# A transformer block on one core: second batch's first feature tiles moved to the end of attention, key rows prepared a product later, weight sums stored in pieces

## The chip, the cores and the metric

The kernel runs on one core of one Trainium2 chip. The core has a matrix engine (PE, whose weight loads are shown as PEld), a vector engine (DVE), an activation engine (ACT), a general engine (POOL) and a synchronization engine (SP), which here only issues DMAs. Each engine runs its own list of instructions in order and waits on semaphores for the others. DMAs are issued by SP, POOL and, a few, ACT; a DMA is in turn on the list of the engine that issues it. The metric is the device time of one execution in microseconds (us), as the median of several runs.

## The reference

The input x has two batches of 2048 tokens with 576 features; a condition vector per batch gives six modulation vectors. All arithmetic is 32-bit.

```python
mod = jax.nn.silu(c) @ w_ada + b_ada
sh_msa, sc_msa, g_msa, sh_mlp, sc_mlp, g_mlp = jnp.split(mod, 6, axis=1)
xn = _ln(x, 1e-06)
xn = xn * (1 + sc_msa[:, None, :]) + sh_msa[:, None, :]
qkv = (xn @ w_qkv + b_qkv).reshape(B, N, 3, H, hd)      # 16 heads of 36
q, k, v = (qkv[:, :, 0], qkv[:, :, 1], qkv[:, :, 2])
q = _ln(q, 1e-05, qn_g, qn_b)
k = _ln(k, 1e-05, kn_g, kn_b)
attn = softmax(jnp.einsum('bqhd,bkhd->bhqk', q, k) * scale)
o = jnp.einsum('bhqk,bkhd->bqhd', attn, v).reshape(B, N, C)
x = x + g_msa[:, None, :] * (o @ w_proj + b_proj)
xn2 = _ln(x, 1e-06) * (1 + sc_mlp[:, None, :]) + sh_mlp[:, None, :]
x = x + g_mlp[:, None, :] * (gelu(xn2 @ w1 + b1) @ w2 + b2)
```

## The kernel before, in words

Tokens are cut into 16 tiles of 128 per batch. For each batch the program projects the tiles to keys, queries and values (`inputs`), runs attention (`attend`), and projects the outputs (`outputs`); behind both batches comes the two-layer MLP. Where a batch's stage ends and the next begins, PE goes straight on.

**The order of the work.** Inside a `tc.manual_schedule(engines=...)` block the named engines run their instructions in the order in which the Python code writes them. Outside of it a scheduler places instructions, and it may place them into an earlier stage if what they need is there. PE is in written order everywhere in this program. In `inputs` DVE, SP and POOL are (for the second batch ACT too); in `attend` DVE, POOL and ACT; around `outputs` DVE alone.

**Feature tiles.** A token tile is normalized, turned by DVE in squares, stored to DRAM (`turned<-squares`, L1034, on POOL) and loaded back with features on the partitions: `input_loaded` (L1042 and two DMAs at L1044 into `xnt`). `input_modulated` then applies scale and shift: four ACT instructions at L1051, one at L388, one at L389, and a subtraction by POOL at L390. For the second batch the rows are turned during the first batch's attention (`turned_early`, at blocks 14 to 29 of its 32). The first three tiles are loaded behind `attend` with `input_loaded(turned.pop(t), nc.sync)`; two are modulated through a table handed to `outputs`, the third in `in_pairs`. That code stands outside of the written order of ACT and SP.

**First batch's projections.** One tile at a time: three products (L1130, L1132), bias additions on DVE (L1145, L1148), and head norms. Each loop over t loads the features of tile t+2 and turns the rows of tile t+3 on POOL's queue, and stores the transposed queries and keys on SP (L1111). At tiles 6 to 11 it also works off the list `summed`: four differences of weight blocks on DVE (`sum_made`, L961), the last rows' difference (`ends_less`), then both stored to DRAM by SP (`sums_kept`, L971 and L972) for the second batch.

**Second batch's projections** (`in_pairs`). Tiles 0 and 1 are projected as above; then seven loops over pairs of tiles, t0 = 2, 4, ..., 14, each with a key, a query and a value product (`seven_products`, L1216 to L1222). A product has four groups of matmuls, (1), (2, 6), (5, 7), (4, 3), each in a PSUM tile of two banks; four such tiles exist. `combined` gives the evictions: `copied` on ACT (L1245) empties group 1, and five DVE instructions `do[0]` to `do[4]` (L1240 to L1244) empty the others: `do[0]` group (2, 6), `do[1]` and `do[3]` group (5, 7), `do[2]` and `do[4]` group (4, 3). `finishing` makes the head norms: squares on ACT (L1279), sums (L1283), roots, reciprocals (L1290), a product on POOL (L1292), the transpose on DVE (L1296) with eight stores (L1299). Behind the keys of every second pair it issues loads of `km` and `ke`, the key rows for attention (`take_k_block`), and behind the queries of the second pair those of `qm` and `qe`; the four DVE instructions that prepare them (L847 twice, L856, L857) go on the list `taken`, which `rows_made` works off.

**Attention.** 8 pairs of heads, 4 blocks of 512 queries, 4 steps each: scores on PE (L1515), exponentials on ACT (L1519), products with the values on PE (L1528), whose sums DVE adds up (L1578, L1580). `hooks` is a table from a step to work to be done there; what a hook returns is done one step later. The last entry of the loop has the step `(None, None, None)`, when the last exponentials are issued.

**Output projection.** PE at L406 and L417, evictions on DVE (L1657, L1670), loads and stores of residual rows on POOL's queue (L1652, L1671), and ACT computing standard deviations (L276) for the first rows of the MLP.

Of the kernel before, what the change touches and what calls it, by code (L numbers as in the profile page):

```python
# [16 lines left out]
P = 128  # L17
# [14 lines left out]
def dit_block(  # L32
# [719 lines left out]
    def block_of_small():  # L752
# [163 lines left out]
        def first_weights(then):  # L916
# [48 lines left out]
                nc.vector.tensor_tensor(raw_less, rows[:, :, 1, :], rows[:, :, 0, :], ALU.subtract)  # L965
                weight_parts(wq4_less, raw_less)

            def sums_kept():
                saved["sums"] = dram.tile([P, 4, 2, 3, HALF], F32, name="sums_kept")
                saved["less"] = dram.tile([P, 3, HALF], F32, name="less_kept")  # L970
                nc.sync.dma_start(out=saved["sums"], in_=sums)  # L971
                nc.sync.dma_start(out=saved["less"], in_=wq4_less.bitcast(F32))  # L972

            by_head = pool.tile([2 * H, HD], F32, name="by_head")
            nc.gpsimd.dma_start(out=by_head, in_=b_qkv[0 : 2 * C].rearrange("(h d) -> h d", d=HD))
# [17 lines left out]
                nc.sync.dma_start(out=saved["wq"], in_=wq[:, :, 0 : 2 * C])  # L993
                nc.sync.dma_start(out=saved["wq4"], in_=wq4.bitcast(F32))

            summed = [*(lambda i=i: sum_made(i) for i in range(4)), ends_less, sums_kept]
            return (wq, wq4, bq), close, (made, ends_made, bias_made, bias_spread, kept, summed)

        def kept_weights():
# [74 lines left out]
        def inputs(b, weights, making, work, xnts, turned, loaded):  # L1074
# [244 lines left out]
            def in_pairs():  # L1319
# [10 lines left out]
                features_begun(3)  # L1330
                k = product(1, 0)
                biased(1, k, 0)
                input_modulated(b, xnts[2])
                q = product(0, 0)
                biased(0, q, 0)
                v = product(2, 0)
# [17 lines left out]
                for t0 in range(2, NT, 2):  # L1354
# [22 lines left out]
                    if not last:  # L1377
                        for t in range(2):
                            input_modulated(b, xnts[t0 + 2 + t])
                        more = token_sums(t0 + 2)  # L1380
                    do[1]()
                    kt()
                    do[2](), do[3](), do[4]()
                    qs, qr, qq, qd, qt = finishing(0, t0)
# [6 lines left out]
                    qd()  # L1391
                    do[1]()
                    if not last:
                        rows_made()
                        rest = [*do[2:], qt]
                        continue
                    key_rows = [*taken]
                    for ready in key_rows[:-2]:
                        ready()
                    qt()  # L1400
                    do[2](), do[3](), do[4]()
                    return key_rows[-2:]

            modulated = {0}
            done = 0
# [315 lines left out]
        for b in range(B):  # L1721
# [42 lines left out]
            if b + 1 < B:  # L1764
                opening["turned"] = {}
                load, measure, root, turn = rows_ahead(lambda t: x[b + 1, t * P : (t + 1) * P, :])

                def turned_early(t):
                    opening["turned"][t] = turn(t)

                def also(block, g, do):
                    at = (*divmod(block, NBLK), g)
                    before = hooks.get(at)
                    hooks[at] = (lambda: (before(), do())[0]) if before else do

                hooks |= {
                    (0, 2, 1): ada_opened,
                    (1, 0, 2): ada_gates,
                    (2, 0, 2): ada_feature_rows,
                    (2, 0, 3): ada_features,  # L1780
                }
                for t in range(NT):
                    also(3 + t // 2, t % 2, lambda t=t: load(t))
                    also(4 + t // 2, 1 + t % 2, lambda t=t: measure(t))
                    also(14 + t, 0, lambda t=t: load(t))
                    also(14 + t, 1, lambda t=t: turned_early(t))
                also(13, 0, root)
            with tc.manual_schedule(
                engines={mybir.EngineType.DVE, mybir.EngineType.Pool, mybir.EngineType.Activation}
            ):  # L1790
# [4 lines left out]
            wp, close_wp = opening["wp"]  # L1795
            if b + 1 < B:
                weights, close_weights, making = kept_weights()
                turned, loaded = opening["turned"], {}
                xnts = {t: input_loaded(turned.pop(t), nc.sync) for t in range(3)}
                first = []  # L1800

                def turned_of(t):
# [1 line left out]
                    return (lambda x1: first.append(squares_turned(x1, nc.gpsimd, squares))) if t <= TPB else None  # L1804

                with tc.manual_schedule(engines={mybir.EngineType.DVE}):
                    outputs(b, wp, {12 + t: [lambda t=t: input_modulated(b + 1, xnts[t])] for t in range(2)}, spare[:8], turned_of)
                close_wp()
                close_outs()

# [383 lines left out]
```

## Time and profile before

| | us |
|---|---|
| median of 3 runs | 3163.59 |
| lowest, highest | 3161.44, 3164.07 |
| profiled execution | 3168.81 |
| its span, first to last instruction | 3167.0 |
| PE busy in the span | 3114.6 |
| DVE, ACT, POOL busy | 1567.3, 1478.1, 709.5 |
| mean granted TensorE clock | 0.994 |

The first batch's projections run until about 245 us, its attention until about 1046, its output projection until about 1118, the second batch's projections until about 1322, its attention until about 2093, then output projection and MLP.

In a timeline each row gives the start, the duration, the engine, the source line, the operation, what it writes and reads, how often it stands there in a row, and in brackets how long the engine was idle before it and what ended that. "b" and "s" are PSUM tiles. Matmuls are pipelined, so the durations of neighbouring rows overlap; the time that a stretch of matmuls takes is read from its start to the next stretch's start. The granted clock is 1.00 where PE runs at full speed.

### The profile page before, as it was taken

The numbers are of one execution on the slowest core, as the hardware profiler recorded it, in microseconds if no ns is written. First come the engines' busy times: TensorE is split into PE (matmuls) and PEld (weight loads), VectorE is DVE, ScalarE is ACT, GpSimd is POOL, SyncE is SP. The second block draws the span as 40 slices with busy tenths as digits, with TensorE's granted clock in tenths as the row PEclk, the third lists the DMA queues.
The fourth block names the chain that finished last, engine by engine and source line by source line (L and its number), as shares of the span: only waits on it lengthen the run. The fifth ranks groups of instructions, "written<-read, shape, count | busy, mean of one in ns | idle before, by whom it ended". The sixth has DMA issues, their size and how long they took to land. (4 is left out here: it accounts for less than half of the span.)

```text
span 3167.0 us, 46995 instructions
## 1 busy us (share of the span) xinstructions
PE 3114.6 (98%) x17511; PEld 1855.1 (59%) x17511; DVE 1567.3 (49%) x2287; ACT 1478.1 (47%) x2853; POOL 709.5 (22%) x996
## 2 busy tenths in 40 slices
PE   8999999989999999999999999999999999999999
PEld 6874333333333677633333333358888888777777
DVE  6773444434443556544344444345566554445454
ACT  2326666666666123366666666643565552000000
POOL 4650110122321345300001111012333320111121
PEclk9999999989999999999999999999999999999999
DMA  5773332233332554511122222146544434333331
GB/s 145 165 163 85 99 90 60 65 85 96 90 95 77 172 126 76 103 43 36 42 59 74 76 61 74 56 148 193 162 133 138 132 111 157 117 120 112 120 105 39
DMA packets 296039, 324.66 MB, mean 103 GB/s; under 512 B 168856, under 2 KB 227032, under 8 KB 293560
## 3 DMA queue, kind: packets, MB, share of 16 engines
q1 hardware_dynamic: 248096, 199.30, 21.7%
q0 software_dynamic: 46528, 116.94, 14.2%
q10 hardware_dynamic: 1176, 5.31, 0.5%
q8 instruction: 141, 2.31, 0.3%
q14 instruction: 98, 0.80, 0.1%
HBM read 200.50 MB, written 110.43 MB: 98 GB/s over the span
## 5 line engine op out<-in xcount | busy, mean ns | idle before, releaser
L1519 ACT ACTIVATE pt<-b 128x512 f32<-128x512 f32 x2048 | 1057.9, 608 | 490.5 <-PE b L1528 272.3
L1528 PE MATMUL b<-pt,vt 128*64 128x512 f32 x4096 | 943.3, 603 | 17.8 <-ACT pt L1519 17.8
L1528 PEld LDWEIGHTS b<-pt,vt 128*64 128x64 f32 x4096 | 273.7, 137 | 606.0 <-issue 444.1
L1515 PE MATMUL b<-qm,km 32*128 32x512 f32 x4096 | 563.9, 613 | 0.6 <-PE b L1515 0.6
L1580 DVE TENSOR_TENSOR ot<-b,ot 128x512 f32<-128x512 f32 x192 | 132.8, 691 | 613.3 <-PE b L1528 613.3
L1515 PE MATMUL b<-qe,ke 16*128 16x512 f32 x2048 | 420.0, 791 | 0.0
L2106 PE MATMUL s<-ws,as 128*128 128x288 f32 x1440 | 351.8, 406 | 0.0
L1515 PEld LDWEIGHTS b<-qm,km 32*128 32x128 f32 x4096 | 191.0, 184 | 272.4 <-ACT pt L1519 211.5
L2106 PEld LDWEIGHTS s<-ws,as 128*128 128x128 f32 x1440 | 273.6, 190 | 75.6
L1130 PE MATMUL s<-wq,xnt 128*128 128x288 f32 x864 | 230.5, 411 | 6.2 <-ACT xnt L1051 4.2
L1547 DVE RECIPROCAL den<-den 128x512 f32<-128x512 f32 x64 | 213.6, 3337 | 12.5 <-DMA den<-den_dram 12.5
L1946 PE MATMUL m<-xnt,wb 128*128 128x256 f32 x864 | 210.5, 379 | 1.8 <-DVE cs L1980 0.9
L1946 PE MATMUL m<-s,wb 128*128 128x256 f32 x864 | 210.0, 379 | 0.0
L1130 PEld LDWEIGHTS s<-wq,xnt 128*128 128x128 f32 x864 | 160.3, 192 | 43.1 <-ACT xnt L1051 4.4
L1578 DVE COPY ot<-b 128x512 f32<-128x512 f32 x64 | 44.3, 692 | 274.1 <-PE b L1528 274.1
L1946 PEld LDWEIGHTS m<-s,wb 128*128 128x128 f32 x864 | 164.2, 190 | 22.3
L1515 PEld LDWEIGHTS b<-qe,ke 16*128 16x128 f32 x2048 | 106.9, 184 | 113.7 <-issue 113.0
L1946 PEld LDWEIGHTS m<-xnt,wb 128*128 128x128 f32 x864 | 158.8, 190 | 21.8 <-DVE cs L1980 1.5
L1051 ACT ACTIVATE xnt<-xnt,mod 128x128 f32<-128x128 f32 x244 | 100.4, 480 | 128.6 <-DMA xnt<-turned 123.1
L1984 ACT ACTIVATE cs<-cs,b_sb 128x512 f32<-128x512 f32 x144 | 98.9, 719 | 112.9 <-DVE cs L1979 89.2
L1034 POOL DMA_DIRECT2D turned<-squares x160 | 107.5, 679 | 192.8 <-DVE squares L1029 180.7
L2106 PE MATMUL s<-ws,hidden 128*128 128x288 f32 x576 | 142.3, 406 | 0.0
(257 smaller groups left out, 3271.8 us busy)
## 6 DMA issues: line engine op xcount, KB each, us to landing
gelu<-cs SPq DMA_DIRECT2D x144, 256.0 KB
hidden<-gelu SPq DMA_DIRECT2D x16, 2304.0 KB
spare<-in_x_dram POOLq DMA_DIRECT2D x64, 288.0 KB, 3.1
x_dram<-spare POOLq DMA_DIRECT2D x64, 288.0 KB, 2.4
qm<-qk SPq DMA_DIRECT2D x256, 64.0 KB
den<-den_dram SPq DMA_DIRECT2D x128, 128.0 KB
xnt<-turned POOLq DMA_DIRECT2D x53, 256.0 KB, 3.9
turned<-squares POOLq DMA_DIRECT2D x160, 72.0 KB, 2.6
```

What stands on the lines that cost most here:

```text
L1034: queue.dma_start(out=by_square[g], in_=squares[g * SQ : (g + 1) * SQ, :].rearrange("p (k j) -> p k j", j=SQ))
L1051: nc.scalar.activation(part, part, AF.Identity, **affine(which, k, b))
L1130: nc.tensor.matmul(out_a, full[:, k, :], wq[:, k, f], start=k == 0, stop=False)
L1515: nc.tensor.matmul(ps, k[r, keys], q[r, :], start=first, stop=not first)
L1519: nc.scalar.activation(pt[:, h, :], banks[2 * c + h], AF.Exp, scale=SCALE)
L1528: nc.tensor.matmul(acc[64 * h : 64 * h + 64, :], vt[:, v0 : v0 + 64], pt[:, h, :], start=pt is pts[0][0], stop=pt is pts[-1][0],)
L1547: nc.vector.reciprocal(den, den)
L1578: nc.vector.tensor_copy(ot, acc)
L1580: nc.vector.tensor_tensor(ot, acc, ot, ALU.add)
L1946: nc.tensor.matmul(out_m[m], wb[:, slot[m], k, f * P : (f + 1) * P], moving[m](k), start=k == 0 and m in (1, 2, 5, 6), stop=k == 1 and m == 1,
L1984: nc.scalar.activation(part, part, AF.Gelu, bias=b1_sb[:, g : g + 1])
L2106: nc.tensor.matmul(ms[m], stationary[m][:, f, :], ws[m][:, f, :], start=(f == 0), stop=(f == HF - 1))
```

## The change

Three edits.

1. The loads of the second batch's first three feature tiles are written as a hook at the last entry of the first batch's attention, on POOL's queue, and one function modulates all three one step later. They are taken out of the code behind attention and out of `in_pairs`.
2. In `in_pairs`, `rows_made` is called in every pair's query product, ahead of the transpose of the keys, and no longer in the value product. Rows whose loads a pair's key product issues are therefore prepared in the next pair's query product.
3. The weight sums are stored in four DMAs, each written one tile behind the sum that it stores, in place of one DMA behind all of them.

```diff
-            def sums_kept():
-                saved["sums"] = dram.tile([P, 4, 2, 3, HALF], F32, name="sums_kept")
-                saved["less"] = dram.tile([P, 3, HALF], F32, name="less_kept")
-                nc.sync.dma_start(out=saved["sums"], in_=sums)
-                nc.sync.dma_start(out=saved["less"], in_=wq4_less.bitcast(F32))
...
-            summed = [*(lambda i=i: sum_made(i) for i in range(4)), ends_less, sums_kept]
+            saved["sums"] = dram.tile([P, 4, 2, 3, HALF], F32, name="sums_kept")
+            saved["less"] = dram.tile([P, 3, HALF], F32, name="less_kept")
+
+            def sum_kept(i):
+                nc.sync.dma_start(out=saved["sums"][:, i], in_=sums[:, i])
+
+            def less_kept():
+                nc.sync.dma_start(out=saved["less"], in_=wq4_less.bitcast(F32))
+
+            summed = [
+                *(lambda i=i: (sum_made(i), i and sum_kept(i - 1)) for i in range(4)),
+                lambda: (ends_less(), sum_kept(3)),
+                less_kept,
+            ]
...
                 biased(1, k, 0)
-                input_modulated(b, xnts[2])
                 q = product(0, 0)
...
                         more = token_sums(t0 + 2)
                     do[1]()
+                    rows_made()
                     kt()
                     do[2](), do[3](), do[4]()
...
                     qd()
                     do[1]()
                     if not last:
-                        rows_made()
                         rest = [*do[2:], qt]
                         continue
-                    key_rows = [*taken]
-                    for ready in key_rows[:-2]:
-                        ready()
                     qt()
                     do[2](), do[3](), do[4]()
-                    return key_rows[-2:]
+                    return taken
...
+                def features_early():
+                    opening["xnts"] = {t: input_loaded(opening["turned"].pop(t), nc.gpsimd) for t in range(3)}
+                    return [lambda: [input_modulated(b + 1, opening["xnts"][t]) for t in range(3)]]
+
+                hooks[None, None, None] = features_early
...
-                turned, loaded = opening["turned"], {}
-                xnts = {t: input_loaded(turned.pop(t), nc.sync) for t in range(3)}
+                xnts, turned, loaded = opening["xnts"], opening["turned"], {}
...
-                    outputs(b, wp, {12 + t: [lambda t=t: input_modulated(b + 1, xnts[t])] for t in range(2)}, spare[:8], turned_of)
+                    outputs(b, wp, {}, spare[:8], turned_of)
```

The order of instructions shows where the scheduler had put the first edit's work, and where it stands now. ACT in the first batch's attention, before (`pt` are the exponentials):

```order
L1519 ACTIVATE pt<-b 128x512 x48
L1051 ACTIVATE xnt<-xnt,mod 128x128 x4
L388 ACTIVATE xnt_8984<-xnt_8984,mod 128x128
L389 ACTIVATE tail<-xnt_8984,mod 128x128
L1519 ACTIVATE pt<-b 128x512 x32
L1051 ACTIVATE xnt<-xnt,mod 128x128 x4
L388 ACTIVATE xnt_8990<-xnt_8990,mod 128x128
L389 ACTIVATE tail<-xnt_8990,mod 128x128
L1519 ACTIVATE pt<-b 128x512 x32
```

and in the changed kernel (where the exponentials are at L1523 and the modulations at L1059):

```order
L1523 ACTIVATE pt<-b 128x512 x600
L1059 ACTIVATE xnt<-xnt,mod 128x128 x4
L388 ACTIVATE xnt_8963<-xnt_8963,mod 128x128
L389 ACTIVATE tail<-xnt_8963,mod 128x128
L1059 ACTIVATE xnt<-xnt,mod 128x128 x4
L388 ACTIVATE xnt_8969<-xnt_8969,mod 128x128
L389 ACTIVATE tail<-xnt_8969,mod 128x128
L1059 ACTIVATE xnt<-xnt,mod 128x128 x4
```

The three groups of modulations, 32 exponentials apart before, now follow the last exponential of the first batch. POOL's list at that place in the changed kernel (L1042 are the stores of turned rows there, L1050 and L1052 the tiles' loads, L1656 and L1675 the output projection's loads and stores):

```order
L1042 DMA turned_8433<-spare 32x18x32 x4
L1050 DMA xnt<-turned_5079 128x4x128
L1052 DMA xnt_8963<-turned_5079 64x128 x2
L1050 DMA xnt<-turned_5302 128x4x128
L1052 DMA xnt_8969<-turned_5302 64x128 x2
L1050 DMA xnt<-turned_5542 128x4x128
L1052 DMA xnt_8975<-turned_5542 64x128 x2
L1656 DMA spare<-x_dram 128x576
L390 TENSOR_TENSOR xnt_8963<-tail,xnt_8963 128x128
L390 TENSOR_TENSOR xnt_8969<-tail,xnt_8969 128x128
L390 TENSOR_TENSOR xnt_8975<-tail,xnt_8975 128x128
L1675 DMA x_dram<-spare 128x576 x2
```

Nine loads and three subtractions have come onto POOL's queue between the last early turned tile and the first stores of the output projection. DVE in the query product of the second pair (t0 = 4), in the changed kernel (L1248 to L1252 are `do[0]` to `do[4]`, L1304 the transpose of the keys):

```order
L1249 TENSOR_TENSOR pair<-s,pair 128x2x288
L847 TENSOR_SCALAR km_217<-km_217,gb_at 64x512
L847 TENSOR_SCALAR ended<-ke_219,gb_at 64x512
L856 TENSOR_SCALAR high<-ended,part_232 64x512
L857 SCALAR_TENSOR_TENSOR ke_219<-ended,part_230,high 64x512
L847 TENSOR_SCALAR qm_218<-qm_218,gb_at 128x512
L847 TENSOR_SCALAR ended<-qe_221,gb_at 128x512
L856 TENSOR_SCALAR high<-ended,part_233 128x512
L857 SCALAR_TENSOR_TENSOR qe_221<-ended,part_231,high 128x512
L1304 STREAM_TRANSPOSE turned_qk<-pair 128x1152
L1250 TENSOR_TENSOR pair<-pair,s 128x288
L1251 TENSOR_TENSOR pair<-pair,s 128x288
```

The key rows stood behind `do[1]` of the value product of the first pair before, and the query rows behind `do[1]` of the value product of the second; now all eight instructions stand in one place.

## The prediction

> **What bounds the kernel now.** I read the page first, then the list of who waited for whom on PE, then stretches of time with their busy time and granted clock, then the timelines of the engines at each wait.
>
> ```profile
> PE 3114.6 (98%) x17511; PEld 1855.1 (59%) x17511; DVE 1567.3 (49%) x2287; ACT 1478.1 (47%) x2853; POOL 709.5 (22%) x996
> ...
> PE b L1528 <- ACT pt L1519: 17.8, 4, 6.7
> PE s L306 <- DVE x_first L283: 9.8, 1, 9.8
> PE s L1216 <- DVE vt L1243: 5.5, 3, 3.0
> PE s L1130 <- ACT xnt L1051: 4.2, 1, 4.2
> ```
>
> PE is busy 3114.6 of 3167.0 us, so the span is PE's list of matmuls plus its idle time of 52.4 us and the time that it runs at a lower clock. None of the three edits removes a matmul. They can win only idle time and low-clock time, and the list names nearly all of it: 17.8 us in attention (L1528; 1.8 of it is at a table load and stays), 5.5 us where the second batch is projected in pairs of tiles (L1216), 4.2 us at the end of the first batch's projections (L1130). The 9.8 us is the start of the program, which no edit touches.
>
> **Edit 1: the second batch's first three feature tiles.** Before, each tile's load stands on SP and its modulation on ACT in the middle of the first batch's attention. Columns of the stretches: length, then busy us (instructions) of PE, PEld, DVE, ACT, POOL, then granted clock, DMA share, GB/s.
>
> ```profile
> 605.93 0.40 SPq L1042 DMA_DIRECT2D xnt<-turned  x1
> ...
> 608.99 1.65 ACT L1051 ACTIVATE xnt<-xnt,mod 128x128 f32<-128x128 f32 x4 [3.33 <-DMA xnt<-turned]
> ...
> 611.94 6.64 PE L1528 MATMUL b<-pt,vt 128*64 128x512 f32 x16 [4.47 <-ACT pt L1519]
> ...
> 620.91:632.89 11.98, 11.98 (x85) 4.39 (x81) 7.18 (x11) 8.27 (x17) 1.89 (x3) 1.00 0.35 108
> 601.42:620.91 19.49, 15.02 (x84) 5.01 (x80) 4.80 (x8) 10.76 (x23) 4.35 (x7) 0.82 0.23 53
> 632.89:652.20 19.31, 14.47 (x85) 4.94 (x81) 4.80 (x8) 10.86 (x23) 4.35 (x7) 0.82 0.22 54
> 664.16:685.85 21.69, 14.97 (x85) 5.07 (x81) 4.82 (x8) 10.78 (x23) 4.12 (x6) 0.76 0.22 52
> ```
>
> The load is issued at 605.93, ACT stands 3.33 us for it and then modulates; the exponentials behind it come late, and PE idles 4.47 us. Each stretch is two attention steps. Two undisturbed steps take 11.98 us; the three disturbed pairs take 19.49, 19.31 and 21.69. That is 7.51 + 7.33 + 9.71 = 24.6 us lost, of which 4.47 + 4.84 + 6.72 = 16.0 is idle (length minus PE busy) and the other 8.5 is the low clock after it (0.76 to 0.82): the matmuls of the row at 611.94 take 6.64 us.
>
> In the changed order the three loads stand on POOL behind the last early turned tile, the modulations on ACT behind the last exponential, and POOL's three subtractions ahead of the first stores of the output projection. What covers them:
>
> ```profile
> 1060.23 0.29 ACT L276 ACTIVATE std<-mv,eps 128x1 f32<-128x1 f32 x1 [15.66 <-DVE mv L274]
> ...
> 1058.86 1.22 POOL L1671 DMA_DIRECT2D x_dram<-spare  x2 [70.65 <-DVE spare L1670]
> ...
> 1117.60 2.10 PE L1130 MATMUL s<-wq,xnt 128*128 128x288 f32 x8
> ```
>
> POOL is idle from 988.2 to 1058.86, ACT for 15.66 us before 1060.23, less than 17 us after the last exponential; the tiles' first reader is PE at 1117.60. Nine loads, by the 605.93 row landed some 3 us after issue, are in well before the last exponential. Three modulations by ACT's stretch at 608.99 (1.65 and two more of a quarter of four, about 2.5 us) are 7.5 us of the 15.66. POOL's subtractions wait for them until about 1052, 7 us before the store they stand ahead of. I take the cost as nothing. Without that cover (loads late by more than 8 us) ACT's standard deviations, the turned rows and POOL's stores come late, PE last. Term: **-24.6 us**.
>
> **Edit 3: weight sums stored one by one.** Before, one store of 3.5 MB is issued at 186.90.
>
> ```profile
> 186.90 0.93 SPq L971 DMA_DIRECT2D sums_kept<-weight_sums  x1
> ...
> 205.64 0.81 POOL L1042 DMA_DIRECT2D xnt<-turned  x1 [10.31 <-DMA turned<-squares]
> ...
> 215.52 0.80 POOL L1042 DMA_DIRECT2D xnt<-turned  x1 [2.40 <-DMA turned<-squares]
> ...
> 220.29 1.65 ACT L1051 ACTIVATE xnt<-xnt,mod 128x128 f32<-128x128 f32 x4 [6.43 <-DMA xnt<-turned]
> ...
> 203.25:212.07 8.82, 8.82 (x43) 7.14 (x41) 2.78 (x3) 1.90 (x5) 6.41 (x8) 1.00 0.91 154
> 212.07:227.60 15.53, 11.33 (x43) 8.66 (x41) 7.37 (x10) 5.41 (x13) 7.30 (x8) 0.78 0.63 115
> ...
> 120.00:160.00 40.00, 40.00 (x183) 32.37 (x182) 34.96 (x47) 11.87 (x27) 21.56 (x26) 1.00 0.56 114
> 186.00:212.00 26.00, 26.00 (x120) 21.00 (x119) 17.27 (x27) 7.02 (x17) 11.58 (x14) 1.00 0.95 239
> ```
>
> From 186 to 212 the DMA engines are 0.95 busy at 239 GB/s. POOL stands 10.31 us for the turned rows of tile 14, issues those of tile 15 late, and tile 15 is modulated at 220.29. Four half products take 8.82 us undisturbed and 15.53 around that wait: 6.7 us, 4.2 of it idle. Now four stores of 0.88 MB go out one tile apart (13.2 us, six half products of 2.2) in the stretch that has 0.56 busy at 114 GB/s; each needs 3.7 us at 239 GB/s, so the share rises to about 0.84. The 10.31 us at 205.64 did not stop PE for tile 14 (the stretch before 212.07 has no idle time), so some 4 us per tile hide under the same slack; SP's three more issues of about 1 us lie on an idle queue. At worst the wait stays (0), at best it goes. I take all of it, since a piece's delay is less than half of one that was hidden. Term: **-6.7 us**.
>
> **Edit 2: key rows prepared in the query product.** Before, four DVE instructions on km and ke stand in the value product, wait for their loads, and hold DVE's last three evictions (L1242 to L1244) of that product; PE needs the banks.
>
> ```profile
> 1160.29:1168.40 8.11, 8.11 (x40) 6.63 (x39) 4.77 (x8) 2.78 (x6) 6.57 (x8) 1.00 0.49 75
> 1168.40:1178.33 9.93, 8.35 (x40) 6.67 (x39) 5.68 (x10) 0.40 (x1) 3.76 (x7) 1.00 0.32 88
> 1218.92:1231.44 12.52, 9.53 (x41) 7.50 (x39) 6.17 (x10) 0.40 (x1) 3.76 (x7) 0.90 0.33 82
> 1272.50:1281.74 9.24, 8.34 (x40) 6.66 (x39) 5.83 (x10) 0.40 (x1) 3.76 (x7) 1.00 0.32 94
> ...
> 1172.44 0.54 DVE L847 TENSOR_SCALAR km<-km,gb_at 64x512 f32<-64x512 f32 x1 [5.55 <-DMA km<-qk]
> ...
> 1174.72 0.44 DVE L1242 TENSOR_TENSOR vt<-vt,s 128x288 f32<-128x288 f32 x1
> ...
> 1184.18 0.76 DVE L1241 TENSOR_TENSOR pair<-s,pair 128x576 f32<-128x576 f32 x1 [0.40 <-PE s L1222]
> 1186.02 1.38 DVE L1296 STREAM_TRANSPOSE turned_qk<-pair 128x1152 f32<-128x1152 f32 x1 [1.09 <-DMA qm<-qk]
> ...
> 1187.77 0.46 DVE L1243 TENSOR_TENSOR pair<-pair,s 128x288 f32<-128x288 f32 x1
> ...
> 1188.79 2.10 PE L1216 MATMUL s<-weight_sums,more 128*128 128x288 f32 x8
> ...
> 1183.87 2.12 POOL L1292 TENSOR_TENSOR pair<-pair,inv 128x1152 f32<-128x1152 f32 x1 [5.56 <-DVE inv L1290]
> ...
> 1187.91 0.46 POOL L390 TENSOR_TENSOR xnt<-tail,xnt 128x128 fp32r<-128x128 f32 x1 [1.50 <-ACT tail L389]
> 1188.32 0.74 POOL L1254 TENSOR_TENSOR more<-xnt 128x256 f32<-128x256 f32 x1
> ...
> 1192.24 2.13 POOL L1292 TENSOR_TENSOR pair<-pair,inv 128x1152 f32<-128x1152 f32 x1 [0.37 <-DVE inv L1290]
> ...
> 1192.97 1.68 DVE L847 TENSOR_SCALAR qm<-qm,gb_at 128x512 f32<-128x512 f32 x1
> ...
> 164.51 5.12 DVE L961 TENSOR_TENSOR weight_sums<-weight_sums,wq 128x864 f32<-128x864 f32 x2
> ...
> 167.35 1.36 POOL L390 TENSOR_TENSOR xnt<-tail,xnt 128x128 fp32r<-128x128 f32 x1
> ```
>
> A product takes 8.11 us; the three after a wait take 9.93, 12.52 and 9.24, together 7.4 us too long (5.5 idle, the rest low clock). That goes: the rows are now asked for some 10 us later than they landed.
>
> What comes: I count from the start T of a query product, 1178.33 for the second pair. DVE is through L1241 at T+6.6, stands 1.09 us ahead of the transpose of the keys, and ends L1243 at T+9.9. The value product's third group (the fifth of the eight matmuls at 1188.79, so about 1189.65) needs that bank at T+11.3 (in the changed program each group follows the same group of the product before): slack 1.4 us. The changed order puts the key instructions between L1241 and the transpose: 1172.44 to 1174.72, 2.3 us, of which 1.1 fill the gap. They begin at T+6.7, while POOL's product of the 1183.87 row runs until T+7.7; beside such a product the instruction at 1192.97 took 1.68 us, where the one at 1172.44 with as many elements to a partition took 0.54, and ended 0.3 after POOL's. That adds 0.7, and a bank is granted 0.1 after its eviction. A key block then costs PE 2.3 - 1.1 + 0.7 + 0.1 - 1.4 = 0.6 us (twice, at the fourth and sixth pair), the last, half-size block 0.1. In the second pair key and query rows are both due, eight instructions, 4.6 us: 2.9 us of stall, and 1.4 of low clock, as behind the 2.99 us wait (12.52 - 8.11 - 2.99). Lower bound: 2.9 + 1.4 + 1.2 + 0.1 = 5.6.
>
> Upper bound: DVE and POOL take turns throughout. At 164.51 two additions took 5.12 us, and POOL's L390, 0.46 at 1187.91, took 1.36 behind them; so the two engines did block each other. Then POOL's two L390 and four token sums of 0.74 each stand between the eight instructions, 3.9 us: a stall of 6.8 and 2.8 of low clock (as over the first stretch in attention, 7.51 - 4.47 = 3.0); 1.5 for each key block, with the two L390; 0.1: 12.7. The collisions in the rows are nearer to that, but not every instruction will meet one: I take **9.8**. Term: -7.4 + 9.8 = **+2.4 us**.
>
> The Trainium skill (SBUF — State Buffer, section SBUF: two separate sides) says that VectorE and GpSimd hold a shared port pair exclusively for a whole instruction. By that rule, the trace agrees: 1.68 us against 0.54 at 1192.97. It would give the upper bound, a rival below.
>
> **Sum.** -24.6 - 6.7 + 2.4 = -28.9. The profiled execution took 3168.8 us (span 3167.0), 5.2 over the median of 3163.6; the difference is taken from the median: 3163.6 - 28.9 = 3134.7.
>
> **Rivals.**
> - No new stall in the query product: the waits go and nothing comes. 3163.6 - 24.6 - 6.7 - 7.4 = 3124.9. For it: 1.4 us of slack and a gap ahead of the transpose. Against: 4.6 us of rows in the second pair.
> - DVE and POOL take turns at every instruction (the skill's rule in full): 3163.6 - 24.6 - 6.7 - 7.4 + 12.7 = 3137.6.
> - The four stores still delay tile 15, since the DMA share of 0.84 is near the 0.95 at which POOL stood: the 6.7 us stays, 3134.7 + 6.7 = 3141.4.
> - The edits to the second batch do not free attention: something else on ACT or SP waits in the places of the three loads. The rows name only these loads; 3163.6 - 6.7 + 2.4 = 3159.3, within 0.2%.
> - Slower: the rows' loads land so late that DVE stands for them in the query product as it did in the value product (5.55 us at 1172.44), with L1242 to L1244 behind it and PE behind those. The key loads landed at 1172.4 and are now needed at T+6.7, about 1185 less the 1.6 that is gone: it decides from some 11 us later than here. Each further us at four places costs four; 13 us eat the whole 38.7 and 13 more: 3177. Against: the loads' order of issue is the same and they have a product more.
>
> **How the numbers follow.** Forecast 50%, no new stall 17%, taking turns 20%, stores still in the way 8%, attention not freed 3%, slower 2%. The range 3124 to 3143 takes in the first four, from the case without new stalls to the stores still in the way; the forecast's own is 3130.5 (9.8 at its lower bound) to 3137.6. About 0.2% (6.3 us) is what a measurement of this kernel can tell: faster 0.95, same 0.03, slower 0.02.
>
> **What would show it.** Right: no wait of L1528 on L1519 beyond the one of 1.8 us at the table load near 571; the row at 220 without its 4.20; waits of L1216 on an eviction of pair, not of vt, the longest in the second pair. Wrong: ACT idle before the modulations after the last exponential, PE idle in the output projection, or POOL waiting for turned rows during tiles 7 to 10.

## The result, and the profile after

The changed kernel takes 3138.63 us (median of 4 runs, 3137.95 to 3139.74) against 3163.30 us of the kernel before on the same chip: ratio 0.9923, 95% interval 0.9906 to 0.9940, so it is faster. The time lies in the predicted range and 3.9 us above the predicted 3134.7. Its profiled execution took 3137.95 us with a span of 3136.0.

The first line of the page of the changed kernel (busy us of each engine):

```profile
PE 3103.5 (99%) x17511; PEld 1853.4 (59%) x17511; DVE 1569.0 (50%) x2287; ACT 1477.0 (47%) x2853; POOL 718.7 (23%) x1005
```

PE does the same 17511 matmuls in 11.1 us less, which is low clock that is gone, and its idle time went from 52.4 to 32.5 us. The list of what PE waited for in the changed kernel (in total, times, longest):

```profile
PE s L306 <- DVE x_first L283: 9.8, 1, 9.8
PE s L1224 <- DVE pair L1251: 3.9, 2, 3.6
PE b L1519 <- issue: 3.0, 1, 3.0
PE s L1138 <- ACT xnt L395: 2.1, 3, 1.0
PE b L1532 <- ACT pt L1523: 1.8, 1, 1.8
```

Of the four waits in attention only the one of 1.8 us at the table load is left; the 4.2 us at the end of the first batch's projections and the waits for `vt` are gone. Two are new: 3.6 us for an eviction of `pair`, as forecast, and 3.0 us ahead of the first scores of the second batch (L1519), which was not.

Lined up matmul by matmul, PE's lists of the two executions run alike to 0.3 us except in four stretches: the program's start, the end of the first batch's projections (tile 15), the middle of the first batch's attention, and the second batch's projections with the first microseconds of its attention. Columns of the stretches here and below: length, busy us of PE, PEld, DVE, ACT, POOL, granted clock, DMA share, GB/s. The last three, before:

```profile
200.56:229.81 29.25, 25.05 (x105) 19.81 (x104) 13.64 (x18) 8.61 (x19) 14.87 (x16) 0.88 0.76 136
589.46:701.40 111.94, 95.91 (x581) 33.67 (x577) 40.69 (x59) 67.97 (x136) 27.24 (x41) 0.89 0.32 84
1158.58:1346.53 187.95, 181.92 (x877) 139.15 (x875) 108.79 (x169) 68.21 (x145) 82.53 (x103) 0.99 0.45 88
```

and the same matmuls in the changed kernel, with a stretch into which two of the four stores of the weight sums moved (issued at 130.81 and 147.89; the others follow at 160.64 and 178.63):

```profile
199.50:222.03 22.53, 22.53 (x104) 18.27 (x103) 14.52 (x20) 9.37 (x20) 11.78 (x12) 1.00 0.60 102
581.67:669.03 87.36, 87.36 (x581) 31.82 (x577) 40.71 (x59) 60.35 (x119) 26.13 (x39) 1.00 0.38 96
1126.35:1315.15 188.80, 181.81 (x877) 140.18 (x875) 110.39 (x169) 68.29 (x146) 84.32 (x103) 0.98 0.45 88
120.00:160.00 40.00, 40.00 (x184) 32.34 (x182) 36.04 (x48) 10.74 (x24) 21.57 (x26) 1.00 0.67 156
```

Between these two executions edit 3 gave 6.7 us, edit 1 24.6 us, edit 2 cost 0.9 us, and the program's start, which no edit touches, gave 1.05 us; 0.4 us were lost in bits elsewhere. That is 31 us, as the spans say (3167.0 - 3136.0). The medians say 24.7. The experiments have two things to explain: where edit 2's cost lies, and why the profiles show some 6 us more than the medians.

### The profile page after: what moved, and what is told of

Same layout as the page of the kernel before. It is cut to its first block, busy times and chain, and to the rows that moved or that the text cites. A ratio compares the mean times of both kernels' runs of the same rounds, so it can differ in the third digit from the quotient of the medians.

```text
span 3136.0 us, 47001 instructions
## 1 busy us (share of the span) xinstructions
PE 3103.5 (99%) x17511; PEld 1853.4 (59%) x17511; DVE 1569.0 (50%) x2287; ACT 1477.0 (47%) x2853; POOL 718.7 (23%) x1005
## 3 DMA queue, kind: packets, MB, share of 16 engines
q0 software_dynamic: 46960, 117.92, 14.4%
## 5 line engine op out<-in xcount | busy, mean ns | idle before, releaser
L1523 ACT ACTIVATE pt<-b 128x512 f32<-128x512 f32 x2048 | 1057.3, 610 | 483.8 <-PE b L1532 267.6
L1519 PE MATMUL b<-qm,km 32*128 32x512 f32 x4096 | 564.0, 615 | 3.0 <-issue 3.0
L1519 PE MATMUL b<-qe,ke 16*128 16x512 f32 x2048 | 421.7, 793 | 0.0
L1519 PEld LDWEIGHTS b<-qm,km 32*128 32x128 f32 x4096 | 192.4, 185 | 272.5 <-ACT pt L1523 210.1
L1519 PEld LDWEIGHTS b<-qe,ke 16*128 16x128 f32 x2048 | 108.1, 184 | 113.5 <-issue 112.7
L1042 POOL DMA_DIRECT2D turned<-squares x160 | 107.5, 679 | 195.9 <-DVE squares L1037 188.2
L1059 ACT ACTIVATE xnt<-xnt,mod 128x128 f32<-128x128 f32 x244 | 100.4, 482 | 101.0 <-DMA weight_sums<-sums_kept 51.4
```

Of the source, the lines that this page charges most:

```text
L1042: queue.dma_start(out=by_square[g], in_=squares[g * SQ : (g + 1) * SQ, :].rearrange("p (k j) -> p k j", j=SQ))
L1059: nc.scalar.activation(part, part, AF.Identity, **affine(which, k, b))
L1519: nc.tensor.matmul(ps, k[r, keys], q[r, :], start=first, stop=not first)
L1523: nc.scalar.activation(pt[:, h, :], banks[2 * c + h], AF.Exp, scale=SCALE)
```

## Experiments

### Each edit alone, and the change without one of them

Four kernels hold parts of the diff. With edit 1 alone:

```diff
-                input_modulated(b, xnts[2])
...
+                hooks[None, None, None] = features_early
...
-                    outputs(b, wp, {12 + t: [lambda t=t: input_modulated(b + 1, xnts[t])] for t in range(2)}, spare[:8], turned_of)
+                    outputs(b, wp, {}, spare[:8], turned_of)
```

> Edit 1 alone, on the kernel before. Between the two profiled executions, edit 1 gives 24.7 us (the lead over the kernel before grows from 7.70 to 32.36 us within attention), edit 3 6.65 us, edit 2 costs 1.0 us net: 30.3 us, and 1.05 us at the very start that no edit touches. But the medians differ by 24.7 us only. Theory (the trace speaks for every execution, and the odd 5.6 us are spread over the program): 24.7 us gained, 3163.3 - 24.7 = 3138.6. Rival (attention was less disturbed in the executions without a profile, and all that is missing is missing here): 24.7 - 5.6 = 19.1 us gained, 3144.2.

Measured: 3143.79 us (5 runs, 3140.42 to 3144.44), ratio 0.9940 (0.9927 to 0.9954), against 3163.06 before in these runs: 19.3 us gained, what the rival said. But its profile has the whole stretch undisturbed:

```profile
198.41:224.30 25.89, 23.07 (x105) 18.29 (x103) 12.40 (x16) 7.96 (x18) 13.97 (x16) 1.00 0.78 142
583.93:671.28 87.35, 87.35 (x580) 31.82 (x576) 40.71 (x59) 60.36 (x118) 26.14 (x39) 1.00 0.38 96
```

The first row is the stretch at tile 15, which this kernel leaves as it was: 25.89 us here where the kernel before took 29.25. Over the 22.53 us without a wait that is 3.4 us instead of 6.7: a wait that no edit had touched cost half as much in this execution.

With edit 2 alone:

```diff
                     do[1]()
+                    rows_made()
                     kt()
...
                     if not last:
-                        rows_made()
...
-                    key_rows = [*taken]
-                    for ready in key_rows[:-2]:
-                        ready()
...
-                    return key_rows[-2:]
+                    return taken
```

> Edit 2 alone. By the profiles: the old waits give 1.6 + 4.9 + 1.1 = 7.5 us back, the new costs are 5.4 us in the second pair, 0.4 and 0.4 behind the fourth and sixth and 2.3 at the start of the second batch's attention, 8.5 us together: 1.0 us slower, 3164.3. By the prediction's price (9.8 - 7.4) 2.4 us slower, 3165.7. Rival (the old waits hang on when DMAs land and are smaller without a profile, so that the missing 5.6 us are here): 6.6 us slower, 3169.9.

Measured: 3162.52 us (11 runs), ratio 1.0002 (0.9993 to 1.0011): no difference, 0.5 us gained by the medians. In its profile the stretch of the pairs takes 188.86 us, like the changed kernel's 188.80.

With edit 3 alone (the functions that issue the stores are those of the diff ahead of the prediction):

```diff
...
-            summed = [*(lambda i=i: sum_made(i) for i in range(4)), ends_less, sums_kept]
+            summed = [
+                *(lambda i=i: (sum_made(i), i and sum_kept(i - 1)) for i in range(4)),
+                lambda: (ends_less(), sum_kept(3)),
+                less_kept,
+            ]
...
```

> Edit 3 alone. By the profiles 6.65 us gained: 3156.7, and the row of tile 15's modulation without its wait of some 4 us on PE. Rival (the wait of PE behind the one large store is in the profiled execution and not in the others; the missing 5.6 us are here): 1.1 us gained, 3162.2.

Measured: 3160.14 us (11 runs), ratio 0.9989 (0.9980 to 0.9998): 2.9 us gained, between the two. The wait at tile 15 is gone, so the mechanism holds; a row of its profile:

```profile
199.30:221.83 22.53, 22.53 (x104) 18.27 (x103) 15.46 (x21) 9.36 (x20) 12.73 (x13) 1.00 0.63 114
```

The change without edit 2, that is, with the lines of the second diff taken back:

> The changed kernel without edit 2 (key rows prepared in the value product, as before). By the profiles edit 2 costs 1.0 us net: 3138.6 - 1.0 = 3137.6, no difference that can be told from the changed kernel. By the prediction's price 3136.2. Rival (old waits smaller without a profile): 3138.6 - 6.6 = 3132.0. In its profile the three waits of the value product's evictions come back (1.6 + 4.9 + 1.1 us with their low clock), and the 3.0 us at the start of the second batch's attention go down to the 1.6 us that the kernel before had there.

Measured: 3138.10 us (5 runs, 3135.96 to 3142.84), ratio 0.9922 (0.9909 to 0.9936). Edit 2 is worth nothing that can be told: 0.5 us against it here, 0.5 us for it above. The prediction's +2.4 was too dear, and the rival's 6.6 falls. In its profile the three waits for `vt` are back, and the wait of 3.0 us ahead of the first scores is gone, so that wait came with edit 2:

```profile
PE s L1224 <- DVE vt L1251: 6.8, 3, 2.8
```

### The kernel before, three more times, and the change without edit 1

To see which part of the time differs between executions, the kernel before was profiled three more times, unchanged, and edit 1's diff was taken back from the changed kernel.

> The kernel before, unchanged, for another profile. Theory: PE's idle time the same within 2 us (52.4 in the first profile; 16.0 in attention), and the execution's length goes with the low clock: about 3163 at a mean clock of 0.995 to 0.996, with less than 18.8 us of low clock, the difference lying behind the attention waits. Rival: attention's 24.6 us again to 0.1 us, and the difference at the other waits (program start, tile 15, the pairs).

> As the run before it: the kernel before, unchanged, for a third profile. Same expectations.

> As the two runs before it: the kernel before, unchanged, for a fourth profile. Same expectations.

Measured: 3165.80, 3162.17 and 3158.25 us, one execution each. With the first profile's 3168.81 their mean is 3163.8, about the median of the unprofiled runs, so a profiled execution is not slower as such; the first was the longest of four. The three stretches of the first repetition:

```profile
199.89:225.85 25.96, 23.07 (x105) 18.28 (x104) 12.62 (x17) 8.18 (x18) 14.00 (x16) 1.00 0.79 143
585.50:694.69 109.19, 94.11 (x581) 33.34 (x577) 40.69 (x59) 67.88 (x136) 27.09 (x41) 0.91 0.34 86
1151.84:1342.77 190.93, 183.13 (x877) 139.99 (x875) 108.18 (x169) 68.22 (x145) 82.64 (x103) 0.98 0.45 87
```

and of the third:

```profile
199.06:224.38 25.32, 23.06 (x105) 18.27 (x103) 12.20 (x16) 7.88 (x18) 13.93 (x16) 1.00 0.79 142
584.03:693.19 109.16, 93.91 (x580) 33.34 (x576) 40.68 (x59) 67.85 (x136) 27.03 (x41) 0.91 0.34 86
1150.33:1335.18 184.85, 180.27 (x877) 138.06 (x875) 108.54 (x169) 68.20 (x146) 82.53 (x103) 1.00 0.46 90
```

Both expectations fail in part. The rival's "attention's 24.6 us again" does not hold: 21.8 us in two of the three (109.19 and 109.16 less 87.35), 15.1 and 15.3 of it idle instead of 16.0, the low clock smaller. The theory's "idle time the same" does not hold in the last two: in all it was 52.6, 49.6 and 48.5 us after 52.4 in the first profile, and most of the difference lies at tile 15 and in the pairs. At tile 15 the wait itself went from 4.2 us to between 1.5 and 2.8: it ends with the landing of a load behind 3.5 MB of stores, and that differs between executions.

> The changed kernel without edit 1 (the three loads and modulations back in the middle of attention). In the profiles of four kernels these places cost 24.6 us each time, 16.0 of it idle and 8.6 low clock; but the medians with and without edit 1 differ by 19.3 (alone) and 22.0 (beside edit 3). Theory (the idle time is the same in every execution, the low clock behind it is not, and a profiled execution has more of it than the median one): some 16 + 5 = 21 us more than the changed kernel, 3159.6, its executions spread over 8 us and more where the changed kernel's spread over 2, the longer ones at a lower mean clock; in its profile again 24.6 us. Rival (edit 1's places cost 24.6 us in every execution, and the odd us of the medians are elsewhere): 3163.2, spread as narrow as the changed kernel's.

Measured: 3158.43 us (11 runs, 3156.57 to 3162.94), ratio 0.9986 (0.9977 to 0.9995); edit 1 is worth 19.8 us beside the other two. That is near the theory's 3159.6, and the rival's 3163.2 falls. But neither's 24.6 us holds: the profile has the attention stretch 22.4 us too long:

```profile
581.42:691.17 109.75, 94.19 (x580) 33.33 (x576) 40.69 (x59) 67.95 (x136) 27.02 (x41) 0.91 0.33 85
```

The lengths of the stretches in all these profiles, in us (the program's start is the time from PE's first matmul to its first at L355):

| kernel | profiled time | program's start | tile 15 | attention | pairs |
|---|---|---|---|---|---|
| before | 3168.81 | 16.6 | 29.25 | 111.94 | 187.95 |
| before, again | 3165.80 | 15.9 | 25.96 | 109.19 | 190.93 |
| before, again | 3162.17 | 14.5 | 24.64 | 111.22 | 187.83 |
| before, again | 3158.25 | 15.1 | 25.32 | 109.16 | 184.85 |
| edit 2 alone | 3168.99 | 15.9 | 29.78 | 111.59 | 188.86 |
| edit 3 alone | 3162.32 | 15.3 | 22.53 | 111.73 | 189.33 |
| edits 2, 3 | 3160.23 | 15.3 | 22.54 | 109.75 | 188.88 |
| edit 1 alone | 3140.42 | 14.4 | 25.89 | 87.35 | 187.64 |
| edits 1, 3 | 3142.84 | 16.6 | 22.53 | 87.36 | 190.90 |
| all three | 3137.95 | 15.6 | 22.53 | 87.36 | 188.80 |

Read down a column, each edit's mean worth comes out: edit 1, seven profiles with a mean of 110.65 against 87.36, 23.3 us; edit 3, six with a mean of 26.8 against 22.53, 4.3 us (2.1 to 7.3); edit 2, seven with a mean of 188.5 (184.85 to 190.93) against three at 188.85, a cost of 0.4 us, which that scatter does not tell from none. Where an edit has acted, the column hardly varies: 22.53 and 87.36 to 0.01 us, 188.80 to 188.88 in the pairs. From the four executions of the kernel before alone: 23.0 + 3.8 - 0.9 = 25.9, and 3163.8 - 25.9 = 3137.9, as the changed kernel's profile has it (3137.95).

By medians edit 1 is worth 19.3, 22.0 and 19.8 us (alone, beside edit 3, beside both), edit 3 2.9, 5.7 and 4.1 (alone, beside edit 1, beside edit 2). For edit 1 the medians stay some 3 us under the profiles. The interval of the first (gain of 14.5 to 23.1 us by its ratio) just misses 23.3. Part of it is chance: the profiled execution of edit 1 alone was the shortest of its five, and its start, tile 15 and pairs lie 2.9 us below the columns' means in sum, of the 3.4 us by which it lies below its median. Why profiles and medians differ beyond that is open.

### Where edit 2's cost lies

The changed kernel's timeline of DVE, then PE, in the second pair:

```profile
1150.81 1.04 DVE L847 TENSOR_SCALAR km<-km,gb_at 64x512 f32<-64x512 f32 x1
...
1154.26 0.95 DVE L847 TENSOR_SCALAR ended<-qe,gb_at 128x512 f32<-128x512 f32 x1
...
1156.12 1.09 DVE L857 SCALAR_TENSOR_TENSOR qe<-ended,part,high 128x512 fp32r<-128x512 f32 x1
1157.13 1.36 DVE L1304 STREAM_TRANSPOSE turned_qk<-pair 128x1152 f32<-128x1152 f32 x1
...
1158.87 0.46 DVE L1251 TENSOR_TENSOR pair<-pair,s 128x288 f32<-128x288 f32 x1
...
1159.47 2.02 PE L1224 MATMUL s<-weight_sums,more 128*128 128x288 f32 x4 [3.59 <-DVE pair L1251]
```

Eight instructions take from 1150.81 to 1157.2, 6.3 us where 4.6 were counted without POOL; the transpose and the fourth eviction follow, and the third group of the value product waits 3.59 us, with the low clock behind it (2.02 us for four matmuls that take 1.13). By the lined-up rows the low clock costs 1.7 us, and the lead over the kernel before falls by 5.4 us there. Two more kernels take that place apart.

In one, only rows whose loads the pair before has issued are prepared, so that the query rows come a pair later:

```diff
+                    due, taken[:] = [*taken], []
...
                     do[1]()
-                    rows_made()
+                    for ready in due:
+                        ready()
                     kt()
```

> The changed kernel with the rows still in the query product ahead of the transpose, but only those whose loads the pair before has issued: the query rows come one pair later, so that no pair has eight. Theory (the 5.4 us of the second pair are those of eight instructions where four fit): second and third pair cost 0.4 us each, 3138.6 - 4.6 = 3134.0; the 3.0 us at the start of attention stay. Rival (it is a collision with POOL's subtractions and token sums, which any four meet): two waits of some 1.5 to 2 us, 3138.

Measured: 3132.94 us (4 runs), ratio 0.9905 (0.9889 to 0.9920), 5.7 us under the changed kernel. There is no wait at that place, in DVE's, POOL's and PE's rows of it:

```profile
1154.15 1.36 DVE L1304 STREAM_TRANSPOSE turned_qk<-pair 128x1152 f32<-128x1152 f32 x1
...
1154.51 0.72 POOL L1262 TENSOR_TENSOR more<-xnt 128x256 f32<-128x256 f32 x1
...
1155.23 2.46 PE L1224 MATMUL s<-weight_sums,more 128*128 128x288 f32 x8
```

Four instructions cost PE 0.4 us (2.46 for eight matmuls that otherwise take 2.10); the 5.4 us are the price of eight.

In the other, POOL's four token sums stand behind the store of the transposed keys, out of the rows' way:

```diff
-                        more = token_sums(t0 + 2)
                     do[1]()
                     rows_made()
                     kt()
+                    if not last:
+                        more = token_sums(t0 + 2)
```

> The changed kernel with POOL's four token sums behind the store of the transposed keys, so that they no longer run beside the eight row instructions. In the changed kernel these took 6.3 us, 4.6 alone. Taking turns in full: 3.0 us of POOL's four sums come off, the wait of 3.6 us goes to 0.6 and its low clock away: 3138.6 - 3.0 - 1.8 = 3133.8. Only partly in each other's way, as the rows show: about 1.1 us comes off, wait 2.5, 3137.5. Rival (no part in it): 3138.6.

Measured: 3136.18 us (5 runs), ratio 0.9919 (0.9905 to 0.9932). Its rows of DVE, POOL and PE:

```profile
1154.11 0.53 DVE L847 TENSOR_SCALAR ended<-qe,gb_at 128x512 f32<-128x512 f32 x1
...
1155.20 0.75 DVE L857 SCALAR_TENSOR_TENSOR qe<-ended,part,high 128x512 fp32r<-128x512 f32 x1
...
1158.25 0.74 POOL L1262 TENSOR_TENSOR more<-xnt 128x256 f32<-128x256 f32 x1
...
1158.21 1.21 PE L1224 MATMUL s<-weight_sums,more 128*128 128x288 f32 x4 [2.48 <-DVE pair L1251]
```

The wait goes from 3.59 to 2.48 us, 1.1 us, which is the smaller of the two sizes on record and not the 3.0 of taking turns in full; and the low clock behind it does not come (1.21 where 2.02 stood), another 1.7 us by the lined-up rows of the two kernels. The query rows' instructions take 0.53 and 0.75 where they took 0.95 and 1.09 beside the sums.

The last kernel of this group concerns the new wait of 3.0 us at the start of the second batch's attention. The changed kernel's rows there, of POOL, DVE and PE:

```profile
1287.31 2.12 POOL L1300 TENSOR_TENSOR pair<-pair,inv 128x1152 f32<-128x1152 f32 x1 [3.85 <-DVE inv L1298]
...
1289.47 1.38 DVE L1304 STREAM_TRANSPOSE turned_qk<-pair 128x1152 f32<-128x1152 f32 x1 [1.63 <-POOL pair L1300]
...
1291.22 0.46 DVE L1251 TENSOR_TENSOR vt<-vt,s 128x288 f32<-128x288 f32 x1
...
1291.78 1.37 PE L1519 MATMUL b<-qm,km 32*128 32x512 f32 x5 [3.00 <-issue]
```

The profile names no releaser ("issue"), but PE starts 0.1 us after the fourth eviction of the last value product ends (1291.68), and that stands behind the transpose of the queries, which waits for POOL. The edit puts the evictions first:

```diff
-                    qt()
                     do[2](), do[3](), do[4]()
+                    qt()
                     return taken
```

> The changed kernel with one edit: in the last value product the three evictions stand ahead of the transpose of the queries. Theory (the 3.0 us at the start of the second batch's attention is a wait for the bank that the fourth eviction empties, which stood 1.4 us and a wait for POOL's product behind the transpose): the wait goes down to about 0.8 us, 3138.6 - 2.2 = 3136.4, and 1.8 us more if the clock stays up. Rival (the 3.0 us is a wait for loads of key or query rows, which come later as SP and POOL now issue them later): the wait stays, 3138.6.

Measured: 3135.43 us (5 runs, 3135.26 to 3136.86), ratio 0.9915 (0.9902 to 0.9929), 3.2 us under the changed kernel: 1.1 us of the wait are left, and the low clock behind it does not come. Rows of DVE and PE:

```profile
1289.23 0.45 DVE L1251 TENSOR_TENSOR vt<-vt,s 128x288 f32<-128x288 f32 x1
...
1289.79 1.28 PE L1519 MATMUL b<-qm,km 32*128 32x512 f32 x5 [1.08 <-issue]
```

The rival, late loads of rows, falls: the order of the loads is the same here, and the wait went with the order of the evictions.

### All of edit 2's cost taken away

Each four row instructions stand in the next pair's key product behind its last eviction, and the last value product's evictions ahead of the transpose:

```diff
+                    due, taken[:] = [*taken], []
...
                     do[2](), do[3](), do[4]()
+                    for ready in due:
+                        ready()
                     ks, kr, kq, kd, kt = finishing(1, t0)
...
                     do[1]()
-                    rows_made()
                     kt()
...
-                    qt()
                     do[2](), do[3](), do[4]()
+                    qt()
                     return taken
```

> The changed kernel, but each group of four row instructions stands in the next pair's key product behind that product's last eviction (never eight at once), and in the last value product the evictions stand ahead of the transpose of the queries. There DVE waits 1.29 us for the squares anyway; of 2.3 us of rows 1.0 delays the sums and with them POOL's product and the transpose of the keys, against 1.4 us of slack. Theory (all of edit 2's new costs come from where the rows stand on DVE: 5.4 us in the second pair, 0.4 + 0.4 in later ones, 2.3 + 0.7 at the start of attention): no wait of a product on an eviction is left, 3138.6 - 9.2 = 3129.4; with only the waits' idle part (3.6 + 0.3 + 0.4 + 3.0) won in a median execution 3131.3. Rival (the slack is smaller than counted, and each of three groups of rows still stalls PE by about 1 us with its low clock of 1.8): 3138.6 - 9.2 + 8 = 3137.

Measured: 3130.06 us (4 runs, 3127.96 to 3130.92), ratio 0.9895 (0.9880 to 0.9910) to the kernel before: between the two sizes of the theory, 8.6 us under the changed kernel, and the fastest version here. The stretch of the pairs, then two rows of PE's waits:

```profile
1128.62:1308.47 179.85, 178.77 (x877) 137.90 (x875) 106.47 (x169) 68.44 (x145) 82.78 (x103) 1.00 0.47 92
```

```profile
PE s L306 <- DVE x_first L283: 9.9, 1, 9.9
...
PE b L1521 <- issue: 1.1, 1, 1.1
```

No product of the projections waits for an eviction any more; the first scores still stand 1.1 us for theirs. 179.85 against 188.80 is 9.0 us, against the mean of 188.5 with the rows in the value product 8.6 us: old place and new place cost alike, and neither was needed.

## Why the prediction was right, and where it was not

**What bounds the kernel** held: PE's idle time and low clock, at the places named. The time was inside the range, but no term had its size, and that they came out 3.9 us apart in sum owes something to luck: edits 1 and 3 were taken too large, edit 2 too dear.

**Edit 1, -24.6.** The mechanism held, and so did the cover. Rows of ACT, then POOL, at the end of the changed kernel's first attention:

```profile
1008.01 3.05 ACT L1523 ACTIVATE pt<-b 128x512 f32<-128x512 f32 x6 [1.04 <-PE b L1532]
1010.88 1.67 ACT L1059 ACTIVATE xnt<-xnt,mod 128x128 f32<-128x128 f32 x4
...
1027.92 0.29 ACT L276 ACTIVATE std<-mv,eps 128x1 f32<-128x1 f32 x1 [8.70 <-DVE mv L274]
...
1018.00 0.46 POOL L390 TENSOR_TENSOR xnt<-tail,xnt 128x128 fp32r<-128x128 f32 x1 [1.85 <-ACT tail L389]
1026.54 1.23 POOL L1675 DMA_DIRECT2D x_dram<-spare  x2 [8.09 <-DVE spare L1674]
```

The modulations follow the last exponentials without a gap, ACT still stands 8.70 us ahead of its standard deviations and POOL 8.09 us ahead of its stores. The size was that of one execution, the longest of seven: 21.8 to 24.6 us, mean 23.3, and 19 to 22 by medians.

**Edit 3, -6.7.** The mechanism held (POOL stood 10.31 us for the turned rows, now 0.53, the longest such wait left there), and the rival that the four stores still delay tile 15 falls in all eight profiles with edit 3 (22.53 or 22.54 us). The DMA share between 120 and 160 rose from 0.56 to 0.67 and not to 0.84, but only two of the stores fall there; in the next 26 us, where the prediction had not looked, the others raised it from 0.60 to 0.78 and, from 173 to 186, from 0.67 to 0.89, and PE lost nothing. The term was too large: 4.3 us on the mean. It was read where the load had landed almost at its latest. The row of POOL in the changed kernel:

```profile
204.67 0.80 POOL L1050 DMA_DIRECT2D xnt<-turned  x1 [0.53 <-DMA turned<-squares]
```

**Edit 2, -7.4 + 9.8.** The sum came out at +0.9 between the first profiles and at +0.4 on the mean, instead of +2.4. The new costs add up to 8.5 us against the forecast 9.8, and that this is near is luck, since the parts lie elsewhere. The second pair cost 5.4 us, nearer to its lower bound of 4.3 than to the 9.6 of taking turns; the fourth and sixth pair 0.4 us each, under even the lower bound of 0.6. The step "the last, half-size block 0.1" is the one that failed: 2.3 us were lost at the first scores behind that block. Rows of DVE in the last pair, first of the kernel before, then of the changed kernel:

```profile
1313.41 1.38 DVE L1296 STREAM_TRANSPOSE turned_qk<-pair 128x1152 f32<-128x1152 f32 x1 [0.71 <-POOL pair L1292]
```

```profile
1279.02 0.80 DVE L847 TENSOR_SCALAR km<-km,gb_at 64x256 f32<-64x256 f32 x1
...
1281.09 1.38 DVE L1304 STREAM_TRANSPOSE turned_qk<-pair 128x1152 f32<-128x1152 f32 x1
```

The block takes DVE 2.1 us, of which 0.7 fill the gap that stood ahead of the transpose of the keys. The prediction counted only what PE's next product waits for, and there the other 1.4 indeed hide. But they make the last evictions of the query product late, with them the squares of the queries, the sums, POOL's product, the transpose of the queries and the evictions of the values, and behind those stand the first scores. One product more along DVE's list shows it. The 1.4 us are read from the rows; how the rest of the 2.3 divides between low clock and scores that had run ahead of the wait before (the kernel before, too, waits there for its fourth eviction, from the third matmul on) is not taken apart.

**The step from profile to median** cost most of the 3.9 us. The prediction set the profiled execution's surplus of 5.2 us aside as a constant, and subtracted from the median waits that had been measured in that execution. But its surplus over the mean of the four lay in those waits: 1.6 us in attention and 3.0 at tile 15, and 1.1 at the program's start. An edit that removes a wait removes its surplus too. On the mean of the four the edits are worth 25.9 us, not 28.9 (edits 1 and 3 are 4.5 smaller, edit 2 is 1.5 cheaper), which leaves 3137.7 from the predicted median and 0.9 us open. In hindsight, the sum of 28.9 taken from the profiled execution's own 3168.8 gives 3139.9, 1.3 us from the result, with edit 2's 1.5 still in it.

**The rivals.** No new stall: falls by the 3.59 us. Taking turns at every instruction: falls by the experiment with the token sums; partly in each other's way is what the rows show. Attention not freed: falls by 87.36. Rows' loads too late: falls, the rows at 1150.81 wait for nothing.

## What to carry to other kernels

A wait that ends with a DMA, and the low clock behind any wait, differ from one execution to the next; before pricing an edit by such a wait, look at it in several profiles, or subtract from the time of the execution in which it was measured. Where instructions are put into an in-order engine's list, follow that list past the next consumer, until the delay has met a gap. And where work with a late deadline waits in one place and crowds in another, spread it: four instructions at a place where their engine idles anyway brought no wait, eight at once cost 5.4 us.

## What was not expected of the hardware

The same wait does or does not bring the low clock. Of the fourteen profiles, two are 1.7 us longer than the others around the table load of the first attention, behind a wait of the same length. Rows of PE in the change without edit 2:

```profile
564.77 5.35 PE L1535 MATMUL b<-pt,vt 128*64 128x512 f32 x16 [1.75 <-ACT pt L1526]
```

and in the changed kernel:

```profile
563.72 3.65 PE L1532 MATMUL b<-pt,vt 128*64 128x512 f32 x16 [1.76 <-ACT pt L1523]
```

The difference is 1.7 us. Behind the 3.59 us of the changed kernel, too, 1.7 us were lost, behind the 2.48 us of the kernel with later token sums nothing. So a wait at these places costs either itself alone or another 1.7 us, and at the first of them its length does not decide which. The Trainium skill (TensorE: Matmul & The Clock Gate, Part 1) says that the clock follows a free-running activity window, so that the loss differs from run to run; the rows here agree in that. In 21 executions of the kernel before, the shortest span was 3156.9 us at a mean clock of 0.997 and the longest 3169.0 at 0.994.

DVE and POOL block each other only in part. Beside the rows' instructions POOL's token sums took 0.79 to 1.17 us, beside the transpose and the evictions (in the kernel with four rows at a time) 0.72, and 0.72 to 0.74 in the kernel with later token sums; the three last instructions on the rows took 0.84 to 1.09 beside the sums and 0.49 to 0.75 without. Full turns, as the rule of the exclusive port pair has it (the Trainium skill, SBUF — State Buffer, section SBUF: two separate sides), would have cost some 3 us by the four sums of 0.72 to 0.74, an estimate; 1.1 were measured, and the measurement decides. The same section limits the rule to VectorE instructions in a two-port mode or with two SBUF inputs; whether all eight are such, no run here shows.
